# Selective-scan layers on one core: one product in four moved from VectorE to GpSimd in the second scan layer

## The chip, the cores and the metric

The kernel runs on one core of a Trainium2 chip. The metric is the device time of one execution in microseconds; the time before is the median of three runs, 15246.63 us (15242.52 to 15286.9). Engines are called by the profile's names: PE (TensorE), DVE (VectorE), ACT (ScalarE), POOL (GpSimd), SP (the queue that issues most DMAs).

## The reference, cut to what matters

Four layers follow each other. The first two are state-space layers; each scans the 4096 tokens of each of 4 images in 4 directions, with 192 channels and 16 states per channel. This is the second layer's scan:

```python
def step(hst, inp):
    x_t, d_t, B_t, C_t = inp
    dA = jnp.exp(d_t[..., None] * A)
    hst = hst * dA + (d_t * x_t)[..., None] * B_t[:, :, None, :]
    y = jnp.einsum('bkdn,bkn->bkd', hst, C_t)
    return (hst, y)
```

`d_t` (dt in the kernel) is a softplus of a projection of the input, `B_t` and `C_t` are projections, and `x_t` is the input. The two other layers (attention, feed-forward) come after the scans and are not touched by the change.

## The kernel before

**Tiling.** One image in one layer is a batch; the batches run in the order of the layers, four of layer one, then four of layer two. A batch has 16 segments: 4 directions times 4 stretches of 1024 tokens. A segment has 192 channels x 16 states = 3072 recurrences, cut into 24 groups of 128 partitions: 6 blocks of 32 channels (`cb`), and in each block 4 groups of 4 states (`sg`). Group number `i` is `4*cb + sg`. Between two batches `side_by_side` finishes one image and starts another; it uses the SBUF tile `area` as scratch, which within a batch holds only the input `xs` of odd segments, in its last two of seven 1024-wide slots.

**One group.** Six engine steps, each over 128x1024 float32 values:

- `spread_u` (L1098, PE, once per block): copies dt*x of the block's 32 channels (`dtu`, SBUF) onto 128 partitions, into the one PSUM tile `u`.
- `decay` (L1105, ACT): `da = exp(A*dt)`, into one of four SBUF buffers; `dts` holds dt spread over 128 partitions, loaded by a broadcast DMA (L1089) from a DRAM copy.
- `enter` (L1109, DVE): `t = u * B`, into one of two PSUM buffers of the ring `ps_t`.
- `recur` (L1116, DVE): the scan `h = da*h + t`, into one of four SBUF buffers. From the second segment of a direction it starts from `state`, which `keep` (L1127, ACT) saved.
- `leave` (L1131, POOL): `hc = h * C`, one of three SBUF buffers.
- `collect` (L1141, PE): four small matmuls add the states of a channel into the PSUM tile `y`.

**Beside them.** While a segment's groups run, `prepare` computes the next segment's dt, B, C and dt*x: transposes (`X`), projections (`P`, L963), a softplus on ACT, sums on PE (`sum`, L1047) with copies on ACT (L1050), and `times` (L1056, POOL), which writes `dtu = dt*x`, twice per segment. B and C go to DRAM and come back spread by 8 broadcast DMAs per segment (L1083).

**Order of the work.** The order on each engine is fixed when the kernel is built, by a planner (`Flow`). Each operation has an estimated cost (1.115 us for `enter`, 2.25 for `recur`, 2.31 for `leave`), dependencies, a due time counted back from its users, and perhaps the mark `hard`. The planner walks simulated time; an operation that is not hard goes ahead of a hard one on its engine only if it ends a guard (4.2 us on PE, 0.5 on the others) before the hard one is due. On the chip each engine then executes its own list in order and waits on semaphores. DVE's list is written out by hand: two `enter`, then their two `recur`, pair after pair, 6.74 us per pair by the planner's costs.

**Zero products.** Where the planner sees PE idle before its next operation it calls `keep_busy`, which issues matmuls of a zero matrix (L1166), one per 0.43 us of the gap, less 2.0 us ahead of a hard operation and 0.1 us ahead of others. They add zeros to the open accumulation of `y`, or, when the last group of a block has been collected (`sg` 3) or no `y` is open, write to a part of `y` that is about to be started anew. PE's clock is granted by the chip, and these products keep PE active.

Of the kernel before, what the change touches and what calls it, by code (L numbers as in the profile page):

```python
# [25 lines left out]
C = 96  # L26
# [3 lines left out]
SEG = 1024  # L30
# [5 lines left out]
GC = 32  # L36
GS = 128 // GC
# [86 lines left out]
class Flow:  # L124

    def __init__(self, fill):
        self.fill, self.ops = fill, []

    def add(self, *args, **kw):
        op = Op(*args, **kw)
# [3 lines left out]
    def run(self):  # L136
        inside = set(map(id, self.ops))
        for op in self.ops:
            op.deps = [d for d in op.deps if id(d) in inside]
            op.left = len(op.deps)  # L140
            for d in op.deps:
                d.users.append(op)
        for op in reversed(self.ops):
            for d in op.deps:
                due = op.due - d.occ - (0.0 if d.engine == op.engine else d.lat)
                d.due = due if d.due is None else min(d.due, due)
        free, ready, hard = {}, {}, {}
        for op in self.ops:
            free.setdefault(op.engine, 0.0)
            ready.setdefault(op.engine, [])  # L150
            if op.hard:
                hard.setdefault(op.engine, []).append(op)
        for ops in hard.values():
            ops.sort(key=lambda op: -op.due)
        for op in self.ops:
            if not op.left:
                ready[op.engine].append(op)
        bank, drift, left, strict = 0.0, 0.0, len(self.ops), True
        while left:
            best = None  # L160
            for engine, ops in ready.items():
                if not ops:
                    continue
                first = hard.get(engine, [])
                while first and first[-1].left < 0:
                    first.pop()
                when = lambda op: max(free[engine], op.seen, op.after, bank if op.bank > 0 else 0.0)
                fits = ops
                if strict and first:
                    limit = first[-1].due + drift - (4.2 if engine == "PE" else 0.5)  # L170
                    fits = [
                        op
                        for op in ops
                        if op.hard or op.due <= first[-1].due or when(op) + op.occ <= max(limit, free[engine])
                    ]
                    if not fits:
                        continue
                soonest = min(map(when, fits))
                if soonest == math.inf:
                    continue  # L180
                op = min((op for op in fits if when(op) <= soonest + 0.1), key=lambda op: op.due)
                if best is None or when(op) < best[0]:
                    best = when(op), op
            if best is None:
                assert strict
                strict = False
                continue
            strict = True
            start, op = best
            engine = op.engine  # L190
            if engine == "PE":
                self.fill(free[engine], start - free[engine] - (2.0 if op.hard else 0.1))
            op.emit()
            left -= 1
            op.left = -1
            ready[engine].remove(op)
            done = op.fin = start + op.occ
            free[engine] = done
            if op.bank:
# [180 lines left out]
class Stream:  # L380
# [516 lines left out]
    def prepare(self, seg, base=0.0, before=None):  # L897
# [157 lines left out]
        def times(half):  # L1055
            nc.gpsimd.tensor_mul(seg.dtu[:, half], v.dt[:, half], seg.xs[:, half])  # L1056

        for half in range(2):
            for j in range(2):
                at = 48.0 + 4.0 * (2 * half + j)  # L1060
                for term in range(4):
                    chain = op(
                        ("sum", half, j),
                        "PE",
                        0.87,
                        partial(add, half, j, term),
                        [chain, o["log"]],
                        at=at + 0.9 * term,
                        lat=0.3,
                        bank=int(term == 0),  # L1070
                    )
                p = chain
                op(("dt", half, j), "ACT", 0.5, partial(keep_dt, half, j), [p], at=at + 4.0, bank=-1)
            done = [o["dt", half, 0], o["dt", half, 1]]
            op(("out", half), "SP", 0.1, partial(out, half), done, at=60.0, lat=3.0)
            op(("u", half), "POOL", 2.31, partial(times, half), done, at=58.0 + 8.0 * half)
        return ops


# [5 lines left out]
    def load_dt(self, seg, cb):  # L1085
# [2 lines left out]
        src = seg.dt_dram.rearrange("h c t -> (h c) t")[cb * GC : (cb + 1) * GC, :]  # L1088
        self.nc.sync.dma_start(seg.dts[cb], src.unsqueeze(1).to_broadcast([GC, GS, SEG]))  # L1089

    def spread_u(self, seg, cb):

        half, blk = divmod(cb, NCB // 2)
        rows = slice(blk * GC, (blk + 1) * GC)
        seg.u = self.k.t(self.ps_u, [128, SEG], "u")
        for j in range(SEG // CH):
            cols = slice(j * CH, (j + 1) * CH)
            self.nc.tensor.matmul(  # L1098
                seg.u[:, cols], self.spread[rows, :], seg.dtu[rows, half, cols], start=True, stop=True
            )  # L1100

    def decay(self, gr):
        gr.da = self.k.t(self.core, [128, SEG], "da", bufs=4)
        scale = gr.seg.bt.lay.neg_a[:, gr.seg.kd, gr.g : gr.g + 1]
        self.nc.scalar.activation(gr.da, gr.seg.dts[gr.cb], AF.Exp, scale=scale)  # L1105

# [4 lines left out]
    def recur(self, gr):  # L1111
# [4 lines left out]
        self.nc.vector.tensor_tensor_scan(  # L1116
            gr.h[:, order], gr.da[:, order], gr.t[:, order], start, op0=ALU.mult, op1=ALU.add
        )

    def keep(self, gr):  # L1120
        seg = gr.seg
# [26 lines left out]
            )  # L1148
        self.open = None if gr.sg == NSG - 1 and cb % 2 else gr

    def keep_busy(self, now, gap):


        lay = self.layers[0]
        if self.open:
            start = self.open.sg == NSG - 1
            half = 1 if start else self.open.cb % 2
# [4 lines left out]
            y, start = self.next_y[:GC, :256], True  # L1162
        else:
            return
        for _ in range(int(gap / 0.43)):
            self.nc.tensor.matmul(  # L1166
                y,
                self.zeros,
# [62 lines left out]
    def batch(self, segs):  # L1231


        slot, length = 6.74, 6.74 * NCB * NSG / 2
        flow, last = Flow(self.keep_busy), segs[-1]
        add = flow.add
        groups = {}
        dve = []

        def put(op, deps=(), due=None, after=0.0):  # L1240
            op.deps += [d for d in deps if d is not None]
# [3 lines left out]
            return op  # L1245

        for n, seg in enumerate(segs):
            base, o, nxt = n * length, seg.o, seg.next
            prev = segs[n - 1] if n else None
            if nxt:  # L1250
                ops = self.prepare(nxt, base, seg)
# [9 lines left out]
                        put(op, free, due=base + 25.0 + at * space, after=base + 10.0 + at * space * 0.8)  # L1261
            for i in range(NG):
                cb, sg = divmod(i, NSG)
                at = base + i // 2 * slot + i % 2 * 1.12
                gr = SimpleNamespace(seg=seg, cb=cb, sg=sg, g=i)
                groups[n, i] = gr
                k0 = n * NG + i
                of = lambda name, back: groups[divmod(k0 - back, NG)].__dict__.get(name) if k0 >= back else None
                if sg == 0:
                    if (n, cb) != (0, 0):  # L1270
# [9 lines left out]
                        "PE",  # L1280
                        1.75,
                        partial(self.spread_u, seg, cb),
                        [of("enter", 1), o.get(("u", cb // 3))],
                        lat=0.25,
                        hard=True,
                    )
                gr.decay = add(
                    "ACT",
                    1.05,
                    partial(self.decay, gr),  # L1290
                    [o.get(("dts", cb)), of("recur", 4), of("decay", 1)],
                    lat=0.2,
                    hard=True,
                )
                gr.enter = add(
                    "DVE",
                    1.115,
                    partial(self.enter, gr),
                    [o["spread", cb], o.get(("load", 0, sg))],
                    lat=0.15,  # L1300
                    due=at,
                    hard=True,
                )
                dve.append(gr)
                if i % 2 == 0:
                    continue
                for g2 in (groups[n, i - 1], gr):
                    k0 = n * NG + g2.g
                    of = lambda name, back: groups[divmod(k0 - back, NG)].__dict__.get(name) if k0 >= back else None
                    start = base + i // 2 * slot + 2.24 + g2.g % 2 * 2.25  # L1310
                    g2.recur = add(
                        "DVE",
                        2.25,
# [34 lines left out]
            if nxt and seg is not last:  # L1348
                for sg in range(NSG):
# [4 lines left out]
                    nxt.o["load", 1, sg] = add(  # L1354
                        "SP", 0.1, partial(self.load_states, nxt, 1, sg), [c, nxt.o["bc_out"]], lat=4.5
                    )
        order = []
        for j in range(0, len(dve), 2):
            order += [dve[j].enter, dve[j + 1].enter, dve[j].recur, dve[j + 1].recur]
        for a, c in zip(order, order[1:]):  # L1360
            c.deps.append(a)
        self.late = flow.run()
# [1076 lines left out]
```

## Time and profile before

| | us |
|---|---|
| median of the runs | 15246.63 |
| the profiled execution, time | 15391.0 |
| the profiled execution, span of the core | 15389.1 |
| four batches of layer one (first to last scan step) | 1322.1, 1326.3, 1312.2, 1319.2 |
| four batches of layer two (first to last scan step) | 1326.0, 1322.4, 1314.2, 1305.5 |
| PE / DVE / ACT / POOL busy over the whole span | 13751.2 / 12831.6 / 8289.2 / 9204.4 |

The batches' bounds come from the times of the first `enter` and the last `recur` of each in the trace. Batches of layer two run at 6504.9 to 7830.8, 7989.0 to 9311.4, 9466.7 to 10780.9 and 10879.8 to 12185.3 us from the span's start. The page's busy shares are means over scans, the work between batches, and the two last layers (from 12.2 ms on), which have other limits; so each stage is read by itself.

### The profile page before, as it was taken

What the parts mean: (1) busy time and instruction counts of PE and PEld (TensorE: products, weight loads), DVE (VectorE), ACT (ScalarE), POOL (GpSimd) and SP (SyncE); (2) the same over time, 40 slices, a digit from 0 to 9 for tenths busy, and PEclk for the clock granted to TensorE, in tenths of its full rate; (3) what the DMA queues carried; (4) which work ended last, traced back from release to release, by engine and by line L of the source; (5) the groups of instructions that cost most, each with busy time, mean ns of one, the idle gap of its engine ahead of it and who ended that gap; (6) DMA issues with size and microseconds to landing.
All of it is one profiled execution on the core that took longest, in us unless ns stands there. A gap on an engine that the chain in (4) does not pass through costs nothing. (4 is left out here: it accounts for less than half of the span.)

```text
span 15389.1 us, 225440 instructions
## 1 busy us (share of the span) xinstructions
PE 13751.2 (89%) x88567; PEld 5562.3 (36%) x88567; DVE 12831.6 (83%) x9645; ACT 8289.2 (54%) x13549; POOL 9204.4 (60%) x4657
## 2 busy tenths in 40 slices
PE   7999899989998999899989998999899889998877
PEld 3333333333333333333333333333333344443344
DVE  1999799969996999699979997999899856565655
ACT  3666466646664666466646665666566423232333
POOL 0898589858985888577747774777577620000123
PEclk9889888878898889888889898888899899998888
DMA  2333433343334333433343334333433400000122
GB/s 79 111 126 125 140 112 126 122 140 112 126 126 139 117 119 127 138 121 114 127 140 123 124 120 146 126 124 111 155 119 119 143 10 11 19 18 13 52 70 71
DMA packets 679264, 1639.33 MB, mean 107 GB/s; under 512 B 102822, under 2 KB 301227, under 8 KB 674428
## 3 DMA queue, kind: packets, MB, share of 16 engines
q1 hardware_dynamic: 641340, 1549.37, 31.7%
q0 software_dynamic: 36864, 75.55, 1.7%
q8 instruction: 700, 11.47, 0.3%
q14 instruction: 360, 2.95, 0.1%
HBM read 1295.03 MB, written 329.58 MB: 106 GB/s over the span
## 5 line engine op out<-in xcount | busy, mean ns | idle before, releaser
L1131 POOL TENSOR_TENSOR hc<-h,bc 128x1024 f32<-128x1024 f32 x3072 | 7203.9, 2363 | 2404.4 <-DVE h L1116 1934.0
L1116 DVE TENSOR_TENSOR_SCAN h<-da,state,t 128x1024 f32<-128x1024 f32 x2304 | 5276.6, 2333 | 30.6 <-ACT state L1127 18.5
L1105 ACT ACTIVATE da<-dts,L_A_logs 128x1024 f32<-128x1024 f32 x3072 | 3510.2, 1149 | 1237.7 <-DVE h L1116 1195.6
L1109 DVE TENSOR_TENSOR t<-u,bc 128x1024 f32<-128x1024 f32 x3072 | 3598.2, 1218 | 281.2 <-PE u L1098 207.5
L1166 PE MATMUL y<-L_diag,zeros 96*32 96x256 f32 x9734 | 2635.8, 410 | 0.0
L1141 PE MATMUL y<-hc,gather_y 128*32 128x256 f32 x24576 | 2434.5, 440 | 35.6 <-POOL hc L1131 34.8
L1098 PE MATMUL u<-dtu,spread 32*128 32x512 f32 x3072 | 1756.5, 696 | 523.9 <-DVE t L1109 517.2
L1116 DVE TENSOR_TENSOR_SCAN h<-da,t 128x1024 f32<-128x1024 f32 x768 | 1711.3, 2270 | 13.0 <-ACT da L1105 8.8
L1166 PEld LDWEIGHTS y<-L_diag,zeros 96*32 96x32 f32 x9734 | 1096.2, 118 | 1418.5 <-issue 664.3
L1141 PEld LDWEIGHTS y<-hc,gather_y 128*32 128x32 f32 x24576 | 723.1, 116 | 1692.2 <-issue 1227.2
L1098 PEld LDWEIGHTS u<-dtu,spread 32*128 32x128 f32 x3072 | 557.2, 201 | 1415.4 <-issue 933.1
L1692 DVE SCALAR_TENSOR_TENSOR hcv<-padv,taps,hcv 128x2048 f32<-128x2048 f32 x384 | 902.2, 2350 | 13.4
L1616 POOL MEMSET padp<- 128x2448 f32 x32 | 68.4, 2137 | 1392.9 <-PE d L1656 1374.8
L1656 PE MATMUL d<-padp,diag 32*32 32x512 f32 x25600 | 885.4, 600 | 2.0 <-ACT hcp L1671 2.0
L1050 ACT COPY dt<-m 96x512 f32<-96x512 f32 x512 | 297.1, 580 | 1056.3 <-PE m L1047 1056.1
L1047 PE MATMUL m<-dtu,ident 96*96 96x512 f32 x1024 | 591.3, 660 | 94.1 <-ACT xs L937 43.8
L963 PE MATMUL m<-area,proj 96*128 96x512 f32 (+1 forms) x1024 | 581.0, 689 | 43.2 <-ACT spare L1195 26.5
L1656 PEld LDWEIGHTS d<-padp,diag 32*32 32x32 f32 x25600 | 481.7, 103 | 372.2 <-issue 198.2
L963 PE MATMUL m<-xs,proj 96*128 96x512 f32 (+1 forms) x1024 | 558.0, 667 | 39.4 <-ACT spare L1195 26.0
L1047 PE MATMUL m<-dt,ident 96*96 96x512 f32 x1024 | 567.0, 637 | 0.0
L1047 PE MATMUL m<-sp_log,ident 96*96 96x512 f32 x1024 | 564.0, 634 | 0.0
L1047 PE MATMUL m<-sp_z,ident 96*96 96x512 f32 x1024 | 551.2, 621 | 0.0
(282 smaller groups left out, 15904.5 us busy)
## 6 DMA issues: line engine op xcount, KB each, us to landing
bc<-bc_dram SPq DMA_DIRECT2D x1024, 512.0 KB
dts<-dt_dram SPq DMA_DIRECT2D x768, 512.0 KB
dt_dram<-dt SPq DMA_DIRECT2D x256, 384.0 KB
y_tok<-spare SPq DMA_DIRECT2D x64, 768.0 KB
dt<-y_tok SPq DMA_DIRECT2D x128, 384.0 KB
x_tok<-area SPq DMA_DIRECT2D x32, 768.0 KB
z_t<-area SPq DMA_DIRECT2D x64, 384.0 KB
area<-x_tok SPq DMA_DIRECT2D x64, 384.0 KB
```

What stands on the lines that cost most here:

```text
L963: nc.tensor.matmul(v.ps, seg.proj[:, src, to], seg.xs[:, src, chunks[j]], start=src == 0, stop=src == 1)
L1047: nc.tensor.matmul(v.ps, k.ident[:C, :C], term[:, half, chunks[j]], start=at == 0, stop=at == 3)
L1050: nc.scalar.copy(v.dt[:, half, chunks[j]], v.ps)
L1098: self.nc.tensor.matmul(seg.u[:, cols], self.spread[rows, :], seg.dtu[rows, half, cols], start=True, stop=True)
L1105: self.nc.scalar.activation(gr.da, gr.seg.dts[gr.cb], AF.Exp, scale=scale)
L1109: self.nc.vector.tensor_mul(gr.t, gr.seg.u, self.bc[:, 0, gr.sg, :])
L1116: self.nc.vector.tensor_tensor_scan(gr.h[:, order], gr.da[:, order], gr.t[:, order], start, op0=ALU.mult, op1=ALU.add)
L1131: self.nc.gpsimd.tensor_mul(gr.hc, gr.h, self.bc[:, 1, gr.sg, :])
L1141: nc.tensor.matmul(seg.y[at : at + GC, cb % 2 * 256 : (cb % 2 + 1) * 256], self.gather_y, gr.hc[:, part * 256 : (part + 1) * 256], start=g ...
L1166: self.nc.tensor.matmul(y, self.zeros, lay.diag.rearrange("p h t c -> p (h t c)")[:, :256], start=start, stop=start, tile_position=(0, 0),)
L1656: nc.tensor.matmul(pc[i][j * 32 : (j + 1) * 32, :], diag[mine, ON_PE.index(t), tap, :], pad[mine, j * 8 + dy : j * 8 + dy + 8, dx : dx + H ...
L1692: nc.vector.scalar_tensor_tensor(to, win, wt, to, op0=ALU.mult, op1=ALU.add)
```

## The change

In layer two alone (`not ordered`), the last group (`sg` 3) of blocks 1 to 4, thus 4 of 24 groups of each segment, is "pooled":

- Its product dt*x*B is made by POOL (`enter_pooled`) instead of DVE. POOL can't read `u` from PSUM, so dt*x goes to DRAM (`u_out`, 2 DMAs per segment) and comes back spread over 128 partitions by a broadcast DMA per pooled group (`load_u`) into slot 0 or 1 of `area`; the product goes into slot 2 or 3.
- Its decays go to PSUM, into a buffer of the ring `ps_t` that is allocated when the block's first group (`sg` 0) has been scanned.
- DVE's list has one `enter` less in these pairs, and the due times follow from a list of times; the next block's `spread_u` waits for the `enter` before the pooled group.
- For layer two, PE's guard is 3.2 us instead of 4.2, and `keep_busy` counts `(gap - 0.15) * 1.4 / 0.43` products, before hard operations too, but none when no `y` is open or its last group has been collected.

The core of the diff:

```diff
-                limit = first[-1].due + drift - (4.2 if engine == "PE" else 0.5)
+                limit = first[-1].due + drift - (self.guard if engine == "PE" else 0.5)
...
-                self.fill(free[engine], start - free[engine] - (2.0 if op.hard else 0.1))
+                self.fill(free[engine], start - free[engine], op.hard)
...
+        def u_out(half):
+            if half == 0:
+                seg.u_dram = k.t(self.dram, [2, C, SEG], "u_dram")
+            nc.sync.dma_start(seg.u_dram[half], seg.dtu[:, half])
...
+            p = op(("u", half), "POOL", 2.31, partial(times, half), done, at=58.0 + 8.0 * half)
+            if not lay.ordered:
+                op(("u_out", half), "SP", 0.1, partial(u_out, half), [p], at=68.0 + 8.0 * half, lat=3.0)
...
+    def load_u(self, gr):
+
+        gr.u = self.area[:, gr.pooled % 2 * SEG : (gr.pooled % 2 + 1) * SEG]
+        src = gr.seg.u_dram.rearrange("h c t -> (h c) t")[gr.cb * GC : (gr.cb + 1) * GC, :]
+        self.nc.sync.dma_start(gr.u, src.unsqueeze(1).to_broadcast([GC, GS, SEG]))
+
+    def enter_pooled(self, gr):
+        at = 2 + gr.pooled % 2
+        gr.t = self.area[:, at * SEG : (at + 1) * SEG]
+        self.nc.gpsimd.tensor_mul(gr.t, gr.u, self.bc[:, 0, gr.sg, :])
...
     def decay(self, gr):
-        gr.da = self.k.t(self.core, [128, SEG], "da", bufs=4)
+        if gr.pooled is None:
+            gr.da = self.k.t(self.core, [128, SEG], "da", bufs=4)
...
+        if gr.ahead:
+            gr.ahead.da = self.k.t(self.ps_t, [128, SEG], "t")
...
+        if dense:
+            count = int((gap - (2.0 if hard else 0.1)) / 0.43)
+        else:
+            count = int((gap - 0.15) * 1.4 / 0.43)
+            if self.open is None or self.open.sg == NSG - 1:
+                return
...
+        pooled = lambda i: not segs[0].bt.lay.ordered and i % NSG == NSG - 1 and 0 < i // NSG < NCB - 1
+        order, times, at = [], {}, 0.0
+        for n in range(len(segs)):
+            for i in range(0, NG, 2):
+                order += [("enter", n, j) for j in (i, i + 1) if not pooled(j)]
+                order += [("recur", n, j) for j in (i, i + 1)]
...
+        dense = segs[0].bt.lay.ordered
+        flow, last = Flow(partial(self.keep_busy, dense=dense), 4.2 if dense else 3.2), segs[-1]
...
-                        [of("enter", 1), o.get(("u", cb // 3))],
+                        [of("enter", 2 if i and pooled(i - 1) else 1), o.get(("u", cb // 3))],
...
+                if pooled(i):
+                    gr.pooled = len(theirs)
+                    theirs.append(gr)
+                    first = groups[n, i - NSG + 1]
+                    first.ahead, there = gr, [first.recur]
+                else:
+                    own.append(gr)
+                    there = [own[-5].recur] if len(own) > 4 else []
...
-                    [o.get(("dts", cb)), of("recur", 4), of("decay", 1)],
+                    [o.get(("dts", cb)), *there, of("decay", 1)],
...
+                if pooled(i):
+                    load = add(
+                        "SP",
+                        0.1,
+                        partial(self.load_u, gr),
+                        [theirs[-3].enter if len(theirs) > 2 else None, o.get(("u_out", cb // 3))],
+                        lat=4.5,
+                    )
+                    gr.enter = add(
+                        "POOL",
+                        2.31,
+                        partial(self.enter_pooled, gr),
+                        [load, o.get(("load", 0, sg)), theirs[-3].recur if len(theirs) > 2 else None],
+                        lat=0.2,
+                        hard=True,
+                    )
```

More of the change, by code (lines that the diff above doesn't have):

```diff
@@ L124, with __init__ @@
 class Flow:
-    def __init__(self, fill):
-        self.fill, self.ops = fill, []
+    def __init__(self, fill, guard):
+        self.fill, self.guard, self.ops = fill, guard, []
     def add(self, *args, **kw):
@@ L1075, in prepare @@
             op(("out", half), "SP", 0.1, partial(out, half), done, at=60.0, lat=3.0)
-            op(("u", half), "POOL", 2.31, partial(times, half), done, at=58.0 + 8.0 * half)
+            p = op(("u", half), "POOL", 2.31, partial(times, half), done, at=58.0 + 8.0 * half)
+            if not lay.ordered:
+                op(("u_out", half), "SP", 0.1, partial(u_out, half), [p], at=68.0 + 8.0 * half, lat=3.0)
         return ops
@@ L1149, in collect, with keep_busy @@
         self.open = None if gr.sg == NSG - 1 and cb % 2 else gr
-    def keep_busy(self, now, gap):
+    def keep_busy(self, now, gap, hard, dense):
         lay = self.layers[0]
+        if dense:
[4 more added lines that the diff above has]
+                return
         if self.open:
@@ L1164, in keep_busy @@
             return
-        for _ in range(int(gap / 0.43)):
+        for _ in range(count):
             self.nc.tensor.matmul(
@@ L1231, in batch @@
     def batch(self, segs):
-        slot, length = 6.74, 6.74 * NCB * NSG / 2
-        flow, last = Flow(self.keep_busy), segs[-1]
+        pooled = lambda i: not segs[0].bt.lay.ordered and i % NSG == NSG - 1 and 0 < i // NSG < NCB - 1
[4 more added lines that the diff above has]
+                order += [("recur", n, j) for j in (i, i + 1)]
+        for x in order:
+            times[x] = at
+            at += 1.12 if x[0] == "enter" else 2.25
+        dense = segs[0].bt.lay.ordered
+        flow, last = Flow(partial(self.keep_busy, dense=dense), 4.2 if dense else 3.2), segs[-1]
         add = flow.add
-        groups = {}
-        dve = []
+        groups, own, theirs = {}, [], []
         def put(op, deps=(), due=None, after=0.0):
@@ L1247, in batch @@
         for n, seg in enumerate(segs):
-            base, o, nxt = n * length, seg.o, seg.next
+            base, o, nxt = times["enter", n, 0], seg.o, seg.next
             prev = segs[n - 1] if n else None
@@ L1263, in batch @@
                 cb, sg = divmod(i, NSG)
-                at = base + i // 2 * slot + i % 2 * 1.12
-                gr = SimpleNamespace(seg=seg, cb=cb, sg=sg, g=i)
+                gr = SimpleNamespace(seg=seg, cb=cb, sg=sg, g=i, pooled=None, ahead=None)
                 groups[n, i] = gr
@@ L1294, in batch @@
                 )
[L1295 to L1304, printed above, removed]
+                if pooled(i):
[14 more added lines that the diff above has]
+                    )
+                else:
+                    gr.enter = add(
+                        "DVE",
+                        1.115,
+                        partial(self.enter, gr),
+                        [o["spread", cb], o.get(("load", 0, sg))],
+                        lat=0.15,
+                        due=times["enter", n, i],
+                        hard=True,
+                    )
                 if i % 2 == 0:
@@ L1309, in batch @@
                     of = lambda name, back: groups[divmod(k0 - back, NG)].__dict__.get(name) if k0 >= back else None
-                    start = base + i // 2 * slot + 2.24 + g2.g % 2 * 2.25
+                    start = times["recur", n, g2.g]
                     g2.recur = add(
@@ L1356, in batch @@
                     )
-        order = []
-        for j in range(0, len(dve), 2):
-            order += [dve[j].enter, dve[j + 1].enter, dve[j].recur, dve[j + 1].recur]
+        order = [groups[n, i].__dict__[kind] for kind, n, i in order]
         for a, c in zip(order, order[1:]):
```

## Prediction

> **What bounds the kernel now.** First the slices of the page, then the groups of instructions with the window set on the four batches of layer two (6504.9 to 12185.3 us), the only place where the instructions change. The page:
>
> ```profile
> DVE  1999799969996999699979997999899856565655
> POOL 0898589858985888577747774777577620000123
> PEclk9889888878898889888889898888899899998888
> ```
>
> Within a batch DVE is at 9 tenths or more; the dips are the work between batches. POOL shows 8 in layer one's batches but 7 in layer two's (slices 17 to 31), which has no gathers on POOL. The groups in the window:
>
> ```profile
> L1131 POOL TENSOR_TENSOR hc<-h,bc 128x1024 f32<-128x1024 f32 x1535 | 3601.2, 2364 | 1484.9 <-DVE h L1116 1225.4 <-PE y L1141 184.2 <-PE m L923 27.1
> L1116 DVE TENSOR_TENSOR_SCAN h<-da,state,t 128x1024 f32<-128x1024 f32 x1152 | 2638.1, 2334 | 0.0
> L1109 DVE TENSOR_TENSOR t<-u,bc 128x1024 f32<-128x1024 f32 x1536 | 1800.1, 1220 | 125.8 <-PE u L1098 125.4
> L1105 ACT ACTIVATE da<-dts,L_A_logs 128x1024 f32<-128x1024 f32 x1532 | 1749.5, 1148 | 636.7 <-DVE h L1116 631.6 <-DMA dts<-dt_dram 2.4
> L1166 PE MATMUL y<-L_diag,zeros 96*32 96x256 f32 x4816 | 1307.2, 412 | 0.0
> ```
>
> The scans wait for nothing (0.0); `enter` waits only for the spread on PE (125.4 of 125.8 us). POOL and ACT wait mostly for DVE. So DVE bounds these batches, PE adds a little, POOL has room. The timeline of DVE gives the beat:
>
> ```profile
> 8565.36 2.34 DVE L1109 TENSOR_TENSOR t<-u,bc 128x1024 f32<-128x1024 f32 x2
> 8567.61 4.58 DVE L1116 TENSOR_TENSOR_SCAN h<-da,state,t 128x1024 f32<-128x1024 f32 x2
> 8572.10 2.34 DVE L1109 TENSOR_TENSOR t<-u,bc 128x1024 f32<-128x1024 f32 x2
> ```
>
> A pair takes 8572.10 - 8565.36 = 6.74 us: two `enter` 2.25 (1.12 each, start to start), two scans 4.49. A batch is 192 pairs, 1294.1 us; the four last 1326.0 + 1322.4 + 1314.2 + 1305.5 = 5268.1, so 5268.1 - 5176.3 = 92 us are stalls (the 125.4 hold the waits ahead of a batch's first `enter` too). About half of them lie in the first segments of the batches. The chain of waits on the page covers only the last layers' end and says nothing here.
>
> **The change, part by part.**
>
> *DVE loses 256 products*: 4 per segment x 16 x 4. By the beat each is 1.116 us: 256 x 1.116 = **-286 us**, all on the bounding engine. A pair with a pooled group takes 5.62 us. Layer one's lists stay as they are, except that its last segment also issues the two u_out DMAs for layer two: nothing.
>
> *The pooled scan* has `da` in PSUM and `t` in SBUF, the other way round than any row. The nearest rows are scans with and without the pointer `state` (2334 and 2271 ns), so an operand's place is bounded by 63 ns either way: 256 x 0.063 = +-16 us. I take 0, as the scan still reads one tensor from each memory.
>
> *ACT's decays into PSUM*: count unchanged (1148 ns each). No row has ACT write PSUM; the nearest, ACT's copies that read it (L1050, 580 ns for 512 columns, against 574 for half a decay), puts the difference within 0.1 us either way, off DVE's path while a decay is in time. What changes is the window: the buffer comes free when `sg` 0 is scanned, and the scan of `sg` 3 starts 2.25 + 1.12 + 2.25 = 5.6 us later, of which 1.15 plus two handovers of 0.2 are used: 4.0 us to spare, where the trace has 8.4 at the median and under 3.5 in 3% of the groups. ACT's copies behind PE's sums (L1050) wait up to 9.9 us in one go, and a decay queued behind such a copy would hold DVE. The planner puts a decay ahead when it is due, so I take 0; the other end is one 2 us stall per segment, 128 us.
>
> *POOL gains 256 products* of 2.36 us (the `leave` row; same shape, all in SBUF): 605 us. A segment's POOL work is 24 + 2 + 4 = 30 operations x 2.35 = 70 us in a segment of 80.9 - 4.5 = 76.4 us, 92%. In one block with a pooled group it is 5 x 2.35 = 11.7 us against DVE's 12.36, so POOL holds its beat; blocks 0 and 5 (13.48 against 9.4) take the two `times`. Cover: four `h` buffers. Today the scan that reuses an `h` starts 8.5 us (median) after its `leave` ended and in no case less than 4.1 (groups 16 to 21, where the sums fill PE). A pooled product ahead of it (2.35) and the shorter pair (1.12) leave 5.0 and 0.7 us. So the usual case costs nothing; if PE's lateness (184 us of POOL's waits, up to 6.3 at once) comes on top, groups 16 to 21 would stall DVE by 1.5 to 3 us per segment, 100 to 190 us. I take 0, as the median margin is seven times the smallest.
>
> *DMA*: per segment 4 loads of 512 KB and 2 stores of 384 KB, 2.9 MB on the 9.5 MB that move now (116 GB/s over 82 us); DMA's share goes from 0.36 to about 0.48. SP issues take 0.5 us each as for `dts`. A load waits in SP's queue for the product two pooled groups back, with `dts` and B/C loads behind it; it then has about 20 us before POOL needs it. ACT's wait for `dts` (2.4 us in the window) says that loads land early. Nothing; the other end, were cover gone, would be one late landing per segment, 64 x 2 us.
>
> *PE: spreads and zeros.* The spread still comes once per block, and the next `enter` still starts two scans (4.5 us) after the `enter` that frees `u`. The four matmul records of a spread take 1.98 us at full clock and 3.78 at half (both in the trace), so DVE stalls if PE is late by over 2.3 or 0.5 us. 25% of the spreads run slow now; 43 of some 380 stalled, by 2.4 us on average. In these batches the clock record shows half clock for 24% of the time, in stretches of 6.8 us at the median, and it fell after 3.4 us windows in which PE was 42 to 87% busy (5th to 95th percentile), not only after idle ones. The change puts 1.4 times the zeros into gaps while `y` is open and none from a block's fourth `collect` to the next block's first, some 3 us shortly before the spread. So I expect half clock for about 35% of the time instead of 24, and stalls in proportion: 92 x 1.5 = 138, **+46 us**. The ends: stalls unchanged (0) and the rival below. Real PE work per segment by the planner's costs, which fit full clock, is 24 x 0.46 + 6 x 1.75 + 16 x 0.87 + 8 x 0.88 + 4 x 0.55 + 3 x 0.5 = 46 us of 76, so throughput holds unless the clock is half for most of the time.
>
> The row on the clock is weighed against the Trainium skill, "TensorE: Matmul & The Clock Gate", section "What's actually happening": it lets the clock fall to half after at least one *idle* window of about 3.4 us. By that rule the 3 us without zeros would never fill a window and PE would stay fast, which would leave the stalls at 92 us and the time at 14961; the windows above fell while half busy, so I go by them.
>
> **The sum**: -286 + 46 = -240 us. The profiled execution (15391.0) is 144 us above the median, a difference that it has with the same instructions; I take the saving as the same in both: 15391 - 240 = 15151 profiled, and 15246.6 - 240 = **15007 us** as the median.
>
> **Rivals.**
>
> *POOL (or ACT) becomes the queue that DVE waits for.* For it: 92% load, 0.7 us left in the tightest groups, `times` falling in the same blocks, the decay's window halved. Against: the beat fits in each block, and margins are 8.5 us mostly. Price 100 to 190 us beside the 46: **15107 to 15197**.
>
> *Slower: PE's clock.* Without zeros at every block's turn the clock drops just ahead of every spread, and the larger count (1.4 times the gap at full clock, 2.8 times at half) stands before the spread when it is cold. Place: `enter` of `sg` 0 waiting for the spread, 384 blocks. Price 2.4 us each. It decides from 286 / 2.4 = 119 more stalled spreads than now, about 160 of 384; at 220 of 384 stalls reach 528 us: 15247 - 286 + (528 - 92) = **15397**. For it: 25% slow spreads with zeros, and only 0.5 us of slack when slow. Against: a slow spread alone still fits, and 1.4 times the zeros fills a window and brings the clock back.
>
> *No effect*: if stalls of both kinds eat 240 to 330 us, within 0.3% (46 us) of the old time, about what a measurement of this kernel tells from no change.
>
> **How the numbers follow.** Forecast 60% (14945 to 15080: no added stall and a scan faster by 16 us, to an added stall of 120); POOL or ACT queue 22%; no effect 5%; slower 13%. The first two are faster: 0.82. The range takes the forecast's own low end, 14940, and most of the first rival: to 15190.
>
> **What would show it.** Right: `enter` x1280 on DVE and x256 of a new POOL line at about 2.36 us in layer two; batches of 1240 to 1270 us; pooled pairs of 5.6 us; DVE's waits still for `u`, POOL near 90% in the batches, granted clock there 0.80 to 0.87. Wrong: scans that wait for POOL's `hc` or for `da` by over 30 us per batch (first rival); over 100 us per batch of waits for `u` (second); pooled products slower than 2.4 us or DVE's scans longer beside them.

## The result, and the profile after

The changed kernel is slower: 15332.83 us against 15255.56 us, a ratio of 1.0047 with a 95% interval from 1.0032 to 1.0061. The forecast was 15007; it failed in sign.

The two profiles side by side mislead at first: the span of the profile after (15320.0) is below that of before (15389.1). The pieces between the batches of layer one explain it: 207 to 216 us in that profile of before, 176 after. No instruction there changed. In all later profiles this piece went with the job in which a kernel ran: 197 to 222 us in two jobs, whatever the kernel, and 173 to 183 in a third; and the kernel before had medians of 15379 and 15399 us in the first two and 15274 in the third. Each of these jobs had another chip, so job and chip can't be told apart. So times are compared only within a job, as ratios, and profiles batch by batch.

The four batches of layer two after. The columns are the stretch and its length in us, the busy time of PE, PE's weight loads, DVE, ACT and POOL with their instructions, the granted clock, DMA's share and GB/s:

```profile
6401.00:7718.50 1317.50, 1250.51 (x5756) 451.04 (x5756) 1235.89 (x704) 825.88 (x1225) 1114.58 (x479) 0.86 0.45 152
7874.70:9193.30 1318.60, 1248.35 (x5744) 450.21 (x5742) 1236.65 (x704) 830.01 (x1230) 1111.57 (x477) 0.86 0.45 152
9354.10:10688.50 1334.40, 1266.17 (x5744) 453.90 (x5743) 1236.94 (x704) 830.65 (x1230) 1111.39 (x477) 0.84 0.45 150
10796.30:12116.30 1320.00, 1249.08 (x5806) 456.84 (x5806) 1235.82 (x704) 809.05 (x1203) 1111.82 (x477) 0.85 0.44 149
```

The first batch of layer two before, in the same view:

```profile
6504.90:7830.80 1325.90, 1227.02 (x5830) 458.29 (x5830) 1289.81 (x768) 829.55 (x1225) 971.41 (x415) 0.88 0.36 116
```

The batches after sum to 5290 us, against 5268 in the first profile of before and 5227 in a second one. DVE has 704 instructions per batch instead of 768, as intended, yet the batches are no shorter. The groups of the batches after:

```profile
L1152 POOL TENSOR_TENSOR hc<-h,bc 128x1024 f32<-128x1024 f32 x1535 | 3595.0, 2362 | 497.3 <-PE y L1162 242.3 <-DVE h L1135 194.3 <-issue 35.3
L1128 DVE TENSOR_TENSOR t<-u,bc 128x1024 f32<-128x1024 f32 x1280 | 1519.3, 1221 | 264.6 <-PE u L1116 222.6 <-DMA bc<-bc_dram 30.5 <-PE m L923 1.6
L1107 POOL TENSOR_TENSOR area<-area,bc 128x1024 f32<-128x1024 f32 x256 | 604.2, 2360 | 293.6 <-DMA area<-u_dram 172.1 <-DMA bc<-bc_dram 112.0 <-DMA u_dram<-dtu 5.4
L1135 DVE TENSOR_TENSOR_SCAN h<-t,state,area 128x1024 f32<-128x1024 f32 x192 | 447.7, 2332 | 39.5 <-ACT t L1124 38.9
L1135 DVE TENSOR_TENSOR_SCAN h<-t,area 128x1024 f32<-128x1024 f32 x64 | 145.5, 2274 | 25.5 <-ACT t L1124 24.9
```

What was moved costs what was forecast: 256 products of 2360 ns on POOL, pooled scans of 2332 and 2274 ns, no longer than the others. What is new are waits: for the spread 222.6 us (125.4 before), for B 30.5 (none before), and of pooled scans for their decays 64 (none before). And there is a loss that no group shows as idle time. The timeline of DVE in a pooled pair and around it:

```profile
8253.61 4.45 DVE L1135 TENSOR_TENSOR_SCAN h<-da,t 128x1024 f32<-128x1024 f32 x2
8258.09 1.23 DVE L1128 TENSOR_TENSOR t<-u,bc 128x1024 f32<-128x1024 f32 x1
8259.46 2.29 DVE L1135 TENSOR_TENSOR_SCAN h<-da,t 128x1024 f32<-128x1024 f32 x1
8261.66 2.26 DVE L1135 TENSOR_TENSOR_SCAN h<-t,area 128x1024 f32<-128x1024 f32 x1
8263.84 2.34 DVE L1128 TENSOR_TENSOR t<-u,bc 128x1024 f32<-128x1024 f32 x2
```

The single product starts at 8258.09 and the scan that reads it at 8259.46, 1.37 us later; in the beat of before, with another product in between, the step is 1.12. The page reports no idle time, as the step lies within what it counts as one instruction following another.

So I count from starts: each step from one DVE instruction to the next in layer two, less its beat (1.12 us behind a product, 2.25 behind a scan). What is left over I call the excess; "late decays" is the excess of scans that wait for ACT's decay. The sums, in us:

| | product to scan | scan to product, no wait | late decays | product waits for u or B | all |
|---|---|---|---|---|---|
| before, two profiles | 6, 6 | -15, -16 | 0, 0 | 110, 70 | 91, 50 |
| after | 66 | 19 | 69 | 245 | 401 |

(The columns left out hold a few us.) The saved products are worth 287 us; the excess grew by 310 to 350.

### The profile page after: what moved, and what is told of

The parts are those of the page before. It is cut to its first block, busy times and chain, and to the rows that moved or that the text cites. A ratio compares the mean times of both kernels' runs of the same rounds, so it can differ in the third digit from the quotient of the medians.

```text
span 15320.0 us, 225429 instructions
## 1 busy us (share of the span) xinstructions
PE 13784.0 (90%) x88339; PEld 5535.7 (36%) x88339; DVE 12630.3 (82%) x9389; ACT 8273.1 (54%) x13549; POOL 9782.1 (64%) x4913
## 5 line engine op out<-in xcount | busy, mean ns | idle before, releaser
L1152 POOL TENSOR_TENSOR hc<-h,bc 128x1024 f32<-128x1024 f32 x3072 | 7197.9, 2362 | 1432.7 <-DVE h L1135 904.4
L1135 DVE TENSOR_TENSOR_SCAN h<-da,state,t 128x1024 f32<-128x1024 f32 x2112 | 4844.8, 2331 | 58.2 <-ACT state L1148 19.3
L1128 DVE TENSOR_TENSOR t<-u,bc 128x1024 f32<-128x1024 f32 x2816 | 3316.0, 1218 | 453.8 <-PE u L1116 338.4
L1124 ACT ACTIVATE da<-dts,L_A_logs 128x1024 f32<-128x1024 f32 x2816 | 3202.3, 1148 | 897.9 <-DVE h L1135 859.9
L1162 PE MATMUL y<-hc,gather_y 128*32 128x256 f32 x24576 | 2494.5, 442 | 47.3 <-POOL hc L1152 45.7
L1135 DVE TENSOR_TENSOR_SCAN h<-da,t 128x1024 f32<-128x1024 f32 x704 | 1572.0, 2270 | 20.9 <-ACT da L1124 8.8
L1107 POOL TENSOR_TENSOR area<-area,bc 128x1024 f32<-128x1024 f32 x256 | 604.2, 2360 | 293.6 <-DMA area<-u_dram 172.1
L963 PE MATMUL m<-xs,proj 96*128 96x512 f32 (+1 forms) x1024 | 660.0, 752 | 62.2 <-ACT dt L976 38.6
L963 PE MATMUL m<-area,proj 96*128 96x512 f32 (+1 forms) x1024 | 663.0, 756 | 49.3 <-ACT dt L976 25.5
L1056 POOL TENSOR_TENSOR dtu<-dt,xs 96x1024 f32<-96x1024 f32 x128 | 301.9, 2359 | 485.2 <-ACT dt L1050 483.3
```

The lines of the kernel that those rows point to most:

```text
L963: nc.tensor.matmul(v.ps, seg.proj[:, src, to], seg.xs[:, src, chunks[j]], start=src == 0, stop=src == 1)
L1107: self.nc.gpsimd.tensor_mul(gr.t, gr.u, self.bc[:, 0, gr.sg, :])
L1128: self.nc.vector.tensor_mul(gr.t, gr.seg.u, self.bc[:, 0, gr.sg, :])
L1135: self.nc.vector.tensor_tensor_scan(gr.h[:, order], gr.da[:, order], gr.t[:, order], start, op0=ALU.mult, op1=ALU.add)
L1152: self.nc.gpsimd.tensor_mul(gr.hc, gr.h, self.bc[:, 1, gr.sg, :])
L1162: nc.tensor.matmul(seg.y[at : at + GC, cb % 2 * 256 : (cb % 2 + 1) * 256], self.gather_y, gr.hc[:, part * 256 : (part + 1) * 256], start=g ...
```

## The experiments

The theory: four separate waits ate the saving, each from one piece of the change: (1) in a pooled pair, product and scan stand next to each other on DVE; (2) the pooled decay's PSUM window is narrow; (3) loads of dt*x hold up the B loads on SP; (4) PE's spreads come late through the new guard and zeros. Rivals: the zeros and the guard alone (then undoing them restores the saving), POOL's load, DMA traffic as such. Late decays, the steps between product and scan, and the excess are counted as in the table. Waits for u and B are the idle times that the group lines print; for u they also hold the waits ahead of a batch's first product, so that before has 125 and 87 us in its two profiles by this count, and after 223. Places in a segment are given by the group number, 0 to 23.

**before_again**: the kernel before.

> The kernel before, unchanged, for a second profile. The first profile's span (15389) is 130 us above the median of the runs, and its pieces between the batches of layer one (207 to 216 us) are longer than those of the changed kernel (176), though nothing there changed. If that was chance, this profile shows about 176 there, a span near 15260, and layer-two batches that sum to 5240 to 5290 us, with stalls of 60 to 110 us. If it is a lasting difference, 210 again. The stalls of layer one's batches show how much they vary with the same instructions: 103 us in the first profile, 140 in that of the changed kernel.

Ratio 1.0006 (0.9984 to 1.0027). The pieces were 200 to 213 us again: not chance but the job, as told above. Layer two summed to 5227 us, excess 50 instead of 91. In layer one excess went from 103 to 126 with the same instructions, so the profiles alone carry some 40 us of doubt per layer.

**old_fill**: zeros and guard as before.

```diff
-        flow, last = Flow(partial(self.keep_busy, dense=dense), 4.2 if dense else 3.2), segs[-1]
+        flow, last = Flow(partial(self.keep_busy, dense=True), 4.2), segs[-1]
```

> The changed kernel, with the zero products and PE's guard of layer two as before (4.2, and the gap less 2.0 or 0.1 us). If the new zeros and the guard made the spreads late, DVE's waits for u in layer two fall from about 243 us of excess back to about 110 and the time to 15333 - 133 = 15200, half clock back to 24%. If the spreads are late because the pairs are shorter and their order on PE is tighter, the waits stay above 200 us and the time at 15300 to 15370.

Ratio 1.0015 (0.9995 to 1.0036), excess 372. Neither side as stated: waits for u fell from 223 to 115 us, within those of before, but waits for B rose from 30 to 82 and late decays from 69 to 89. Most of the loss is not the zeros' or the guard's. The half-clock share, the part of a batch in which PE had half its clock, was 0.28 to 0.32 with 850 to 930 zero records in a batch, against 0.29 to 0.31 with 1112 to 1222 in the changed kernel.

**fill_alone**: the kernel before with the new zeros and guard.

```diff
-        pooled = lambda i: not segs[0].bt.lay.ordered and i % NSG == NSG - 1 and 0 < i // NSG < NCB - 1
+        pooled = lambda i: False
...
-            if not lay.ordered:
+            if False:
```

> The kernel before, with only the new zeros and guard in layer two: no pooled products, no copies of dt*x. If the zeros and the guard are to blame: about 15256 + 100 to 130 = 15370, with DVE's waits for u in layer two at 200 to 240 us. If they are harmless or a help: 15230 to 15280. The rule that the clock falls only after an idle window expects no change in the half-clock share (24%); my count of the windows before a fall expects about 29%, as the changed kernel showed.

Ratio 1.0061 (1.0042 to 1.0081): they cost some 90 us by themselves. Waits for u were 213 us, 82 of them at group 8; the half-clock share was 0.25 to 0.27 against 0.20 to 0.24 in the two profiles of before. DVE's products in this run:

```profile
L1128 DVE TENSOR_TENSOR t<-u,bc 128x1024 f32<-128x1024 f32 x1536 | 1798.9, 1217 | 213.0 <-PE u L1116 212.7
```

**guard_old**: the changed kernel with the old guard, and the new zeros.

```diff
-        flow, last = Flow(partial(self.keep_busy, dense=dense), 4.2 if dense else 3.2), segs[-1]
+        flow, last = Flow(partial(self.keep_busy, dense=dense), 4.2), segs[-1]
```

> The changed kernel with PE's guard at 4.2 us as before, but with the new zeros. In the changed kernel 42 of 64 spreads ahead of group 8 were late (124 us), with the projection's matmuls ahead of them on PE; with the old zeros and guard together 14 us. If the guard is what lets these matmuls in front, the waits at group 8 fall below 30 us here too, and those with 10 to 14 zeros in front (group 12, 23 us) stay. If the zeros are what makes the spread late, group 8 stays above 80 us. The ratio goes from 1.0047 to 1.000 to 1.003 in the first case.

Waits at group 8 went from 124 us to 8: it was the guard, which lets the projection's matmuls (L963) in front of the spread. A late spread in the changed kernel, which also ran at half clock (3.77 us):

```profile
8480.88 2.02 PE L963 MATMUL m<-xs,proj 96*96 96x512 f32 x2
8482.83 1.08 PE L1162 MATMUL y<-hc,gather_y 128*32 128x256 f32 x8
8483.85 3.77 PE L1116 MATMUL u<-dtu,spread 32*128 32x512 f32 x4
8487.66 1.23 DVE L1128 TENSOR_TENSOR t<-u,bc 128x1024 f32<-128x1024 f32 x1 [5.39 <-PE u L1116]
```

With the new zeros kept, waits for u were 107 us. The waits at group 12, which were expected to stay, fell too, from 25 us to 3; of those that are left, 75 us lie at group 20 (19 in the changed kernel, 14 and 1 before), and no run shows why. The products also waited for B now: 100 us instead of 30. Ratio 1.0025 (1.0011 to 1.004).

**swap_old**: the pooled scan ahead of its neighbour's, old zeros and guard.

```diff
-                order += [("recur", n, j) for j in (i, i + 1)]
+                order += [("recur", n, j) for j in ((i + 1, i) if pooled(i + 1) else (i, i + 1))]
```

> The changed kernel with the old zeros and guard, and DVE's order in a pooled pair turned from (enter, its scan, pooled scan) to (enter, pooled scan, its scan). Theory: a scan right behind the product that it reads starts 1.37 us after it instead of 1.12, 0.25 us x 256 = 66 us in layer two. These go to below 10 us. The decay of the pooled group has 2.25 us less, so its lateness, 89 us, grows: to 130 to 200 us. Together a ratio of 1.0015 to 1.006. If the 0.25 us is no dependence but the cost of a change of operands' memories, they stay.

The excess of the step from product to scan fell from 66 us to 10; the decays' lateness rose from 89 to 185. The dependence is shown:

```profile
8200.65 1.23 DVE L1128 TENSOR_TENSOR t<-u,bc 128x1024 f32<-128x1024 f32 x1
8201.79 2.28 DVE L1135 TENSOR_TENSOR_SCAN h<-t,area 128x1024 f32<-128x1024 f32 x1
8203.99 2.26 DVE L1135 TENSOR_TENSOR_SCAN h<-da,t 128x1024 f32<-128x1024 f32 x1
```

Product to scan is 1.14 us now, and the product's own scan comes third. Ratio 1.0019 (1.0003 to 1.0035): one cost exchanged for the other.

**da_sbuf**: pooled decays in the four SBUF buffers, so both tensors of the pooled scan come from SBUF.

```diff
-        if gr.pooled is None:
-            gr.da = self.k.t(self.core, [128, SEG], "da", bufs=4)
+        gr.da = self.k.t(self.core, [128, SEG], "da", bufs=4)
...
-        if gr.ahead:
-            gr.ahead.da = self.k.t(self.ps_t, [128, SEG], "t")
...
-                    first.ahead, there = gr, [first.recur]
+                    there = [of("recur", 4)]
...
-                    there = [own[-5].recur] if len(own) > 4 else []
+                    there = [of("recur", 4)]
```

> The changed kernel, with the decays of the pooled groups in the four SBUF buffers, as those of the other groups; so the scan of a pooled group reads both its tensors from SBUF. If the narrow window in PSUM is what makes these scans wait, their waits for ACT (70 us) go, and with them the 0.1 us by which an enter waits for the scan just before it that frees its PSUM buffer (26 us): 15333 - 96 = 15237. If a scan with both tensors in SBUF gets in the way of POOL, whose products run beside it, the pooled scans or POOL's products get longer than 2.33 and 2.36 us; at twice the scan's time 256 x 2.3 = 590 us are lost: up to 15830.

Both halves came true. Late decays went from 69 us to 0. The products of groups 6, 10, 14 and 18 take a PSUM buffer that the scan just ahead of them frees in the changed kernel, and here don't: their step behind that scan fell from 2.34 us to 2.22, the value of before, which is 30 us over 256 steps. But pooled scans and POOL's products slowed each other down:

```profile
L1149 POOL TENSOR_TENSOR hc<-h,bc 128x1024 f32<-128x1024 f32 x1536 | 3912.9, 2567 | 635.0 <-DVE h L1134 361.0 <-PE y L1159 198.4 <-DVE t L1127 24.8
L1134 DVE TENSOR_TENSOR_SCAN h<-da,state,area 128x1024 f32<-128x1024 f32 x192 | 710.0, 3698 | 0.0
L1134 DVE TENSOR_TENSOR_SCAN h<-da,area 128x1024 f32<-128x1024 f32 x64 | 229.0, 3578 | 0.0
```

A scan takes 3.6 to 3.7 us instead of 2.3, some 304 us of excess in all, and POOL's `hc` 2567 ns on average instead of 2362. Ratio 1.0163 (1.0132 to 1.0194). So, of these two ways, decays in PSUM are the cheaper one, even with their narrow window.

**no_product**: the pooled products left out, old zeros and guard.

```diff
-        self.nc.gpsimd.tensor_mul(gr.t, gr.u, self.bc[:, 0, gr.sg, :])
```

> The changed kernel with the old zeros and guard, with the pooled products left out: POOL does nothing for them, and the pooled scans read what lies in that tile. Everything else stays, the copies of dt*x too. If POOL's 605 us of extra work make its other products late, and so PE's collects and the spreads queued behind them, DVE's waits for u (96 us) and for decays (89 us) fall towards those of the kernel before (70 and 0), and the ratio to 0.995 or less. If POOL has room, as the margins of the h buffers say, the time stays within 0.2% of the kernel with the products: 0.9995 to 1.0035.

Ratio 0.9992 (0.9974 to 1.0011), just under the range stated for room on POOL and far from 0.995. The excess was 371 against 372 with the products (old_fill); waits for u 112 against 115, late decays 76 against 89, and waits for B 105 against 82. With the products the same job gave 1.0014 (late_load, below): some 34 us more, with intervals that overlap, and 9 us more of excess. So POOL's load is not the cause of the loss, beyond that much.

**late_load**: the planner counts more time for the stores of dt*x, old zeros and guard.

```diff
-                op(("u_out", half), "SP", 0.1, partial(u_out, half), [p], at=68.0 + 8.0 * half, lat=3.0)
+                op(("u_out", half), "SP", 0.1, partial(u_out, half), [p], at=68.0 + 8.0 * half, lat=8.0)
```

> The changed kernel with the old zeros and guard, and one number changed: the planner counts 8 us instead of 3 until the stores of dt*x have landed, so that the loads of dt*x stand behind the B and C loads on SP's queue, not in front of them. Theory: SP waits up to 6 us for the store to land (477 us in all) with the B loads behind it, and the first products of a segment wait for B (82 us of DVE). Then these waits fall below 15 us, SP's wait for the store below 100 us, and the ratio to the kernel before goes from 1.0015 to 0.997. Rival: B is late because of the added traffic itself; then DVE's wait for B stays at 50 to 90 us and the ratio at 1.0015.

This one tells nothing of the cause: the order on SP came out the same as in old_fill, issue for issue. It serves as a second profile of old_fill: the ratio, 1.0014 (1.0000 to 1.0029), repeats old_fill's, and the excess is 380 against 372.

**b_first**: guard_old, with the loads of dt*x behind the B loads.

```diff
-                        [theirs[-3].enter if len(theirs) > 2 else None, o.get(("u_out", cb // 3))],
+                        [theirs[-3].enter if len(theirs) > 2 else None, o.get(("u_out", cb // 3)), o.get(("load", 0, NSG - 1))],
```

> The changed kernel with the old guard and the new zeros, and the loads of dt*x made to depend on the last B load of the segment, so that they stand behind all B loads on SP's queue (the planner's 8 us did not move them). Theory as before: the B loads wait behind a load that waits for its store to land. DVE's wait for B at group 0 (100 us with the old guard) falls below 15 us and the ratio by 0.004 to 0.006, from 1.0025 to about 0.998. Rival, the traffic itself: 70 to 110 us stay, ratio 1.002 to 1.003.

The waits for B went from 100 us to nothing that the groups show, the excess from 356 to 237, and the ratio to 0.992 (0.9899 to 0.9941), more than expected. DVE's products in guard_old and then in b_first:

```profile
L1128 DVE TENSOR_TENSOR t<-u,bc 128x1024 f32<-128x1024 f32 x1280 | 1518.4, 1219 | 216.8 <-PE u L1116 106.8 <-DMA bc<-bc_dram 100.2 <-PE y L1162 0.5
```

```profile
L1128 DVE TENSOR_TENSOR t<-u,bc 128x1024 f32<-128x1024 f32 x1280 | 1514.4, 1221 | 105.8 <-PE u L1116 97.5
```

SP's queue in old_fill, at the turn of a segment:

```profile
8239.08 0.58 SPq L1061 DMA_DIRECT2D u_dram<-dtu  x1
8245.04 1.17 SPq L1102 DMA_DIRECT2D area<-u_dram  x2
8246.26 1.24 SPq L1090 DMA_DIRECT2D bc<-bc_dram  x2
```

and in b_first:

```profile
8155.59 0.58 SPq L1061 DMA_DIRECT2D u_dram<-dtu  x1
8157.12 1.65 SPq L1090 DMA_DIRECT2D bc<-bc_dram  x2
8162.14 0.31 SPq L1053 DMA_DIRECT2D dt_dram<-dt  x1
8163.85 1.81 SPq L1090 DMA_DIRECT2D bc<-bc_dram  x3
8165.76 1.21 SPq L1102 DMA_DIRECT2D area<-u_dram  x2
```

In the first the load waits 5.4 us for its store, with two B loads behind it; in the second the B loads go 1 us after the store. SP's wait for that store (us in total, times, longest), in guard_old and then in b_first:

```profile
SPq L1102 <- DMA u_dram<-dtu: 481.4, 108, 6.5
```

```profile
SPq L1102 <- DMA u_dram<-dtu: 104.3, 48, 3.6
```

The copies and their bytes are the same, so it is the queue's order and not the traffic.

**early**: guard_old, with the pooled decays due about 2 us earlier.

```diff
+                    due=times["recur", n, i] - 4.2 if pooled(i) else None,
```

> The changed kernel with the old guard and the new zeros, with the pooled groups' decays due 2 us earlier for the planner, as soon as their PSUM buffer is free, so that ACT's softplus work and the copies that wait for PE go behind them. Theory: the pooled scans' wait for ACT (78 us with the old guard, at groups 7 and 11 above all, behind softplus steps) falls below 25 us, ratio 1.0025 to about 0.999. If the decay is late because its buffer comes free late, not because of what stands before it on ACT, 60 us or more stay.

The decays' lateness fell from 78 to 29 us as the theory has it: what stood before them on ACT (softplus steps, themselves behind copies that wait for PE) made them late. But the ratio rose to 1.0053 (1.0034 to 1.0071): waits for u went from 107 to 212 us and for B from 100 to 117. A reading that no run tests: work on ACT that had been let in front now came late for PE.

**b_early**: both edits.

> Both of the last two edits. If the two causes are independent, the gains add: 100 + 55 us from the changed kernel with the old guard, a ratio of 0.993 to 0.996. If DVE only waits elsewhere instead (the spread on PE at group 20, 73 us), 0.998 or more.

Ratio 0.9931 (0.9912 to 0.9951), no better than b_first: decays 22 us instead of 76, waits for u 142 instead of 98. The second gain did not add. The ratio lies in the range stated for gains that add only because b_first alone had gained more than expected.

**all3**: both edits and the turned order.

> Both edits, and the pooled scan ahead of its neighbour's on DVE, which took the 66 us of a scan behind its own product away and cost 95 us more of late decays. With the decays due when their buffer is free, the late decays should cost under 80 us here: a ratio of 0.990 to 0.996, the best of the versions. If a decay can't be ready in the 3.4 us that the turned order leaves it, 120 us or more of waits for ACT stay, and it is no better than the version with both edits alone.

Ratio **0.9871** (0.9850 to 0.9891), the best: 15206.99 us against 15398.73 for the kernel before in the same job. Excess 197 (239 in b_early): product to scan 8, decays 84, waits for u 111 (142 in b_early). The planner came out with 1584 to 1712 zero records in a batch, and the half-clock share fell to 0.10 to 0.14; that may be part of the gain, and no run parts it from the turned order's. Of the 86 us that this run's median lies below b_early's, the profiles show 41 in layer two and 28 outside it, where no instruction changed.

## Why the prediction was wrong, step by step

The sign failed in two ways: the removal was priced by the beat alone, and three terms beside it (decays, DMA, PE) were put at nothing or too low.

- *DVE loses 256 products, 286 us "by the beat"*: the count and the size of a product were right. The failed step is pricing the removal by the beat alone. The beat of 1.12 held because two products and two scans alternate, so that no instruction follows the one it reads or whose buffer it takes. With one product in the pair, two such steps appear: product to its scan, 60 us, and scan to the product that takes its PSUM buffer, 34 us (the table's differences). The first was shown by swap_old, the second by da_sbuf (30 of the 34).
- *Decays into PSUM, taken as 0 with 128 us as the other end*: 69 us. The window of 4.0 us to spare was worked out rightly; "the planner puts a decay ahead when it is due" was wrong for the chip, where softplus steps and copies stood ahead on ACT, and the copies waited for PE's projections (early). Of the 69 us, 61 lie at groups 7 and 11.
- *POOL, taken as 0*: right (no_product; no DVE wait on POOL's `hc` shows in layer two after). POOL was 83 to 85% busy. The POOL half of the first rival fell, its ACT half came at about half its price.
- *DMA, "nothing"*: 30 us in the changed kernel, 82 to 100 once the guard was undone. The failed step is looking at SP's wait for the buffer of the pooled product and not at its wait for the store of dt*x to land, with B loads behind it (b_first).
- *PE, +46 us*: after, products waited 245 us by the table against 110 and 70; without B's 30 that is +105 to +145. The size failed, and in part the reason: 124 us lie at group 8 and come from the guard (guard_old), which the prediction did not price. The half-clock share rose to 0.29 to 0.31 (forecast 0.35), but old_fill has the same share and half the waits. Nor did the zeros grow by 1.4 in sum: a batch has 1112 to 1222 zero records after and 1182 to 1270 before, since those between blocks went.
- *The clock*: in the 3.4 us ahead of a fall within the batches, PE was 27 to 87% busy before and 33 to 85% after (5th to 95th percentile), with medians of 63 and 71%. The prediction's low end of 42% was misread: it is the 25th percentile of a count that takes in the pieces between the batches, whose 5th is 13. The Trainium skill, "TensorE: Matmul & The Clock Gate", section "What's actually happening", puts the clock at half after at least one idle window of about 3.4 us, by which no change was to be expected here. The trace shows one (0.24 to about 0.30), and the measurement decides.

By the sum: -287 + 60 + 34 + 69 + 30 + 105 to 145 = +11 to +51, beside +77 measured. The rest, 26 to 66 us, stays open; two profiles of the same kernel differ by 41 in layer two alone. The sum sorts the lost time of one profile by kind; what a single edit gives back is another number, since undoing one wait lengthened others (old_fill, guard_old, swap_old, early). The slower rival, which asked for 119 more stalled spreads, had the right sign and one part of the right mechanism, stalled spreads: 111 waits for u after against 48 (the prediction has 43) and 42 before, so some 65 more, and the other waits made up the rest.

## What to carry to other kernels

An instruction on a saturated engine is worth its beat only if what closes up behind it is independent: look at which neighbours become producer and consumer, or share a buffer, when one goes. A load that reads back what was just stored stalls an in-order DMA queue until the store has landed, and whatever stands behind it; put it behind loads that are ready. Where a planner fixes the engines' lists, each executed in order, a change of one guard or due time moves the waits elsewhere, so read all waits of the bounding engine after each edit, not the one that was meant.

## What the runs showed of the hardware

- A DVE scan that read both tensors from SBUF beside running POOL products took 3.6 to 3.7 us on average (up to 6.8) instead of 2.3, with POOL's `hc` products 9% longer (2567 ns against 2362); with one of the two in PSUM neither showed it.
- A DVE instruction that reads what the one just ahead of it wrote started 0.25 us later than with one other in between (1.37 us against 1.12), and one that overwrites what the one just ahead of it read about 0.1 us later (2.34 against 2.22).
- ACT's decays took 1110 ns into PSUM against 1145 into SBUF.
- A store of 384 KB and the load that waits for it, on the same queue, were issued 6 us apart in the stretch shown, with nothing in between; the 108 waits of this kind in guard_old took 4.5 us on average.
